# Gathering id blocks one tile a slot instead of four at once, in a graph layer followed by a mixture of experts

## The chip, the cores and the metric

The kernel runs on one core of a Trainium2 chip. The core has five engines, each with an instruction queue of its own that it works off strictly in order: TensorE (PE; its weight loads are listed as PEld), VectorE (DVE), ScalarE (ACT), GpSimd (POOL) and SyncE (SP, which only issues DMAs here). Engines wait for each other, and for DMAs, by semaphores. The metric is the device time in microseconds. The time before is 1313.23 us, the median of three runs (1313.06 to 1322.8).

## The reference

6250 nodes with 256 features, 100000 edges with 96 features. `dst` names the node that each edge belongs to, and it is sorted. What is computed, cut to what matters:

```python
x1 = layernorm(x)
s, c, m = segment_sum(edge, dst), count(dst), segment_max(edge, dst)   # per node, 0 where c is 0
h = concat([x1, s, m, s / max(c, 1), u[0]])
x = x + relu(h @ W1 + b1) @ W2 + b2 + x1                                # 1024 hidden
y = layernorm(x)
top2 of y @ gate_w + gate_b; weights = softmax(top2 values)
moe = sum over the two experts of weight * (relu(y @ w1[e] + b1[e]) @ w2[e] + b2[e])
out = x + layernorm(y + moe) * gamma + beta
```

All of it is float32.

## The kernel before

**Tiles and groups.** The nodes are cut into 50 tiles of 125, and these into 13 groups: group 0 has two tiles, the others four. Groups go from the last nodes to the first. For each group the kernel builds the transposed input `inT` (`turn`), runs the hidden layer (`hidden`, L766 and L771, eight column blocks) and the output layer (`output`, L779), adds the residual, normalizes (`norm_b`, L806, into the tile `xr`), transposes that for the gate (`turn_b`, L818), picks two experts (`choose`, `rank`, `rank_2`, `place`) and sends each row twice to its expert's place in DRAM (`send`, L891, indirect DMAs on GpSimd: eight for a group of four tiles). `xr` has one buffer, so `norm_b` of a group can write only when the sends of the group before have been read out. The experts' blocks come after all groups, from about 815 us on.

**The edge stream.** The sums and maxima per node come from running sums over the sorted edges. VectorE makes them in chunks (L316 to L320, with ScalarE copying the first item of a region, L312 and L313); SyncE loads the edges (`raw`, L176, three buffers) and stores the running sums (`rows_d`, L329). The edges lie in seven regions. The stores of region 0 go to an address that comes from a register. Over the ends of runs a small chain is made (`over_runs`, `over_partitions`, `to_runs`), whose result GpSimd writes to `carry_d` (L440). A group then gathers its nodes' rows of `rows_d` (`take_edges`, L722, tile `at`) and of `carry_d` (`take_carry`, L729, tile `cg`), with indirect DMAs on GpSimd, and VectorE joins the two (L735 and L737). `keep_x` has a part on ScalarE (L714) and then one on GpSimd (L716).

**The node search.** To know which row of `rows_d` a node needs, the kernel finds the first edge of each node in two steps. `find_block(t)` (L486, ScalarE) compares the nodes of a tile with the first ids of 400 blocks of 250 ids and counts. `take_blocks(a, z)` turns the counts of tiles a to z into block numbers (L490 to L492, three VectorE instructions) and gathers, for each of those tiles, one block of 250 ids for each node (L495, one indirect DMA a tile on GpSimd, tile `gb`, six buffers). `find_edge(t)` (L502, ScalarE) counts within the block. `bounds`, `index_nodes` and `counts` then make the indices. Groups are searched in batches: batch 2 is group 2 (4 tiles), batch 3 is group 3 plus one more (8 tiles), batch 4 has 12 tiles, batch 5 has 20. Batches 0 and 1 are done in the prologue.

**The order of the work.** It is written out by hand. Each task is given a slot with `at_slot`; a group has twelve slots (`SLOTS`), and group g begins in slot 12 g. Tasks are emitted by slot, within a slot in the order in which they were added, and each engine runs its instructions in the order in which they were emitted. A slot is not a time: an engine goes on as soon as its semaphores allow. Between slots, as much of the edge stream is emitted as a credit of 4.6 us a slot allows, less the `cost` that tasks name. For a batch with first slot U, the lines around the change are

```python
for i, t in enumerate(reversed(range(a, z))):
    if b > GW:
        at_slot(U + i, find_block, t)
    at_slot(U + i + GS + 3, find_edge, t)
for t0 in range(z - GS, a - GS, -GS):
    t1 = t0 + GS
    at_slot(U + z - t1 + GS, take_blocks, max(t0, a), t1, cost=0.5)
```

with GS = 4, and U = 0, 6, 26 and 54 for batches 2 to 5. So four gathers each are emitted in slot 4 (batch 2), 10 and 14 (batch 3), 30, 34 and 38 (batch 4), 58, 62, 66, 70 and 74 (batch 5). The tasks of the groups are added before those of the search, so they come first within a slot. GpSimd's other tasks are: `fill_rows` (slot 4, added last; two DMAs of 2088 KB that preset the experts' rows), `keep_x` of groups 1 to 7 (slots 5, 20, 29, 41, 53, 65, 77), `take_edges` and `take_carry` of groups 2 to 7 (from slots 17, 26, 38, 50, 62 and 74 on, over three slots each, two tiles a slot), and `send` of groups 0 to 4 (slots 23, then 35 and 36, 47 and 48, 59 and 60, 71 and 72).

Of the kernel before, what the change touches and what calls it, by code (L numbers as in the profile page):

```python
# [11 lines left out]
I32 = mybir.dt.int32  # L12
# [7 lines left out]
P = 125  # L20
# [9 lines left out]
KB = 250  # L30
GS = 4
# [13 lines left out]
def kernel(  # L45
# [18 lines left out]
    nc = tc.nc  # L64
# [114 lines left out]
    ix = edges.enter_context(tc.tile_pool(name="ix", bufs=1, side="right"))  # L179
# [46 lines left out]
    def load_all_ids():  # L226
        L = L100
        nc.vector.memset(ids100[:, L:], N)
        src = bass.AP(tensor=dst.tensor, offset=dst.offset, ap=[[L, 100], [1, L + WE]])
        nc.scalar.dma_start(ids100[0:99], src[0:99])  # L230
        nc.scalar.dma_start(ids100[99:100, 0:L], src[99:100, 0:L])
# [19 lines left out]
    def limits():  # L251

        nc.vector.tensor_scalar(low, part_i[:100], float(ER // L100), float(P * GRP[GW - 1][0]), op0=OP.is_equal, op1=OP.mult)
        nc.vector.memset(limit, 2.0 * N)
        at_p = ix.tile([100, 1], F32, name="at_p")
        for c in range(len(JR) - 1):
            lo, q = P * GRP[GW + sum(GR[:c + 1]) - 1][0], REG[c][0] // L100 - 1
            assert REG[c][0] % L100 == 0
            nc.vector.tensor_scalar(at_p, part_i[:100], float(q), float(lo - 2 * N), op0=OP.is_equal, op1=OP.mult)
            nc.vector.tensor_add(limit, limit, at_p)  # L260

    def check_order():

        L = L100
        nc.vector.tensor_tensor(viol[:, 0, :], ids100[:, 0:L], ids100[:, 1:L + 1], op=OP.is_gt)
        nc.vector.tensor_tensor(viol[:, 1, :], ids100[:, 0:L], ids100[:, WE:L + WE], op=OP.is_equal)
        nc.vector.scalar_tensor_tensor(viol[:, 1, :], ids100[:, 0:L], float(P * GRP[GW - 1][0]), viol[:, 1, :],
                                       op0=OP.is_ge, op1=OP.mult)

    def check_fit():  # L270
        L = L100
        red = ix.tile([100, 3], F32, name="red")
        nc.vector.tensor_reduce(red[:, 0:1], viol.rearrange("p h k -> p (h k)"), AX.X, OP.max)
        nc.vector.tensor_tensor(red[:, 1:2], ids100[:, L - 1:L], limit, op=OP.is_ge)
        nc.vector.tensor_tensor(red[:, 2:3], ids100[:, 0:1], low, op=OP.is_lt)
        ps_v = eps.tile([P, 3], F32, name="ps")
        nc.tensor.matmul(ps_v, ones[:100, :P], red, start=True, stop=True)
        bad = ix.tile([P, 1], F32, name="bad")
        nc.vector.tensor_reduce(bad, ps_v, AX.X, OP.add)
        nc.vector.tensor_scalar(misfit, bad[0:1, :], 1.0, None, op0=OP.min)  # L280
        nc.vector.tensor_scalar(shift, bad[0:1, :], 1.0, float(EP * JR[0]), op0=OP.min, op1=OP.mult)
        nc.vector.tensor_scalar(nf, bad, 0.0, None, op0=OP.is_equal)
# [168 lines left out]
    def block_starts():  # L451
        nc.vector.tensor_copy(dsf, ids100[:, 0:E // 100].rearrange("p (q k) -> p q k", k=KB)[:, :, 0])
        nc.vector.tensor_tensor(dsx, ident[:100, None, :100].to_broadcast([100, QB, 100]),
                                dsf[:, :, None].to_broadcast([100, QB, 100]), op=OP.mult)
        ps_b = eps.tile([P, NBK], F32, name="ps")
        nc.tensor.matmul(ps_b, ones[:100, :P], dsx.rearrange("p q k -> p (q k)"), start=True, stop=True)
        nc.scalar.copy(b1r, ps_b)
# [5 lines left out]
    blk_i = ix.tile([P, NT], I32, name="blk_i")  # L463
# [4 lines left out]
    def more_constants():  # L468
        nc.vector.tensor_scalar(nhalf, node_i, -0.5, None, op0=OP.add)
        nc.vector.memset(rp[:, NT:], float(E))  # L470
        nc.vector.tensor_scalar(sh, row_i[:P, :P], 1.0, part_i[:P], op0=OP.add, op1=OP.is_equal)
        nc.vector.tensor_scalar(wrap, row_i[:P, :P], float(P - 1), None, op0=OP.is_equal)
        nc.vector.tensor_scalar(wrap, wrap, ident[:P, 0:1], None, op0=OP.mult)
        nc.vector.tensor_scalar(before, row_i, part_i, None, op0=OP.is_gt)
        nc.vector.memset(cnt_f, 0.0)
        nc.vector.memset(M[:, 0, :], 0.0)

    dst_b = dst.rearrange("(b k) -> b k", k=KB)

    def node_cols(b):  # L480
        g0 = sum(IB[:b])
        return GRP[g0 + IB[b] - 1][0], GRP[g0][1]

    def find_block(t):
        junk = ix.tile([P, NBK], BF16, name="junk")
        nc.scalar.activation(junk, b1r, AF.Sign, scale=-1.0, bias=nhalf[:, t:t + 1], accum_out=acc1[:, t:t + 1])  # L486

    def take_blocks(a, z):
        cols = slice(a, z)
        nc.vector.tensor_scalar(blk_f[:, cols], acc1[:, cols], float(NBK), 0.5, op0=OP.add, op1=OP.mult)  # L490
        nc.vector.tensor_scalar(blk_f[:, cols], blk_f[:, cols], -1.0, 0.0, op0=OP.add, op1=OP.max)
        nc.vector.tensor_copy(blk_i[:, cols], blk_f[:, cols])  # L492
        for t in reversed(range(a, z)):
            gbs_[t] = ix.tile([P, KB], I32, name="gb", bufs=6)
            nc.gpsimd.indirect_dma_start(out=gbs_[t], out_offset=None, in_=dst_b,  # L495
                                         in_offset=IndirectOffsetOnAxis(ap=blk_i[:, t:t + 1], axis=0))

    gbs_ = {}

# [659 lines left out]
    def at_slot(T, fn, *a, cost=0.0):  # L1159
        tasks.append((T, len(tasks), fn, a, cost))  # L1160
# [85 lines left out]
    for b in range(GW, len(IB)):  # L1246

        a, z = node_cols(b)
        U = max(0, SLOTS * (sum(IB[:b]) - 1) - 10 - (z - a))
# [3 lines that stand above are left out]
            at_slot(U + i + GS + 3, find_edge, t)  # L1253
        for t0 in range(z - GS, a - GS, -GS):
            t1 = t0 + GS
            at_slot(U + z - t1 + GS, take_blocks, max(t0, a), t1, cost=0.5)
        T = max(0, SLOTS * sum(IB[:b]) - (9 if b == GW else 12))
        at_slot(T, bounds, b, cost=0.4)
        at_slot(T + 1, index_nodes, b, cost=4.0)
        at_slot(T + 1, counts, b, cost=1.0)  # L1260
# [13 lines left out]
    def loads_1():  # L1274
        take_x(0)
        nc.sync.dma_start(w1x, w1[0:KC * 128].rearrange("(k p) h -> p k h", p=128))
        for q in range(4):
            nc.sync.dma_start(w1r[q * KR:(q + 1) * KR],
                              w1[KC * 128:KC * 128 + KR].rearrange("k (j m n) -> k m j n", m=4, n=128)[:, q])
        take_x(1)  # L1280
        load_ids(0)

    def loads_2():
        nc.gpsimd.dma_start(w1u, w1[D + 3 * EF:D + 3 * EF + GF])
        nc.gpsimd.dma_start(u0, u[0:1].rearrange("a g -> g a"))
        nc.gpsimd.dma_start(b1c, b1.rearrange("(k p) -> p k", p=128))
# [15 lines left out]
    a, z = GRP[0]  # L1302
    a1, z1 = GRP[1]
# [5 lines left out]
    with tc.manual_schedule():  # L1309
        load_all_ids()  # L1310
        loads_1()
        nc.gpsimd.memset(base[0], 0.0)
        loads_2()
        more_constants()
        limits()
        nc.scalar.copy(gap, eps_t[0:1])
        nc.vector.memset(fill, 0.0)
        block_starts()
        check_order()
        for t in reversed(range(a, z)):  # L1320
            find_block(t)
        take_blocks(a, z)
        for t in reversed(range(a1, z1)):
            find_block(t)
        check_fit()
        take_blocks(a1, z1)
        bad_v = nc.values_load(misfit[0:1, 0:1])
    with tc.If(bad_v != 0):

# [163 lines left out]
```

## Time and profile before

| what | value |
|---|---|
| median of three runs | 1313.23 us |
| the profiled execution | 1304.08 us |
| its span, first to last instruction | 1302.3 us |
| PE busy | 1134.1 us (87%) |
| DVE busy | 929.0 us (71%) |
| ACT busy | 646.4 us (50%) |
| POOL busy | 591.3 us (45%) |
| id gathers, L495 POOL, x50 | 67.9 us, 1359 ns each |
| sends, L891 POOL, x100 | 133.4 us, 1334 ns each |
| searches, L502 ACT, x50 | 500 ns each (median) |
| id gathers, from issue to landing | 3.9 / 6.1 / 9.4 us (least, median, most) |

How to read it: the profile gives one execution. Its slices show the busy share of each engine in 40 equal parts of the span, in tenths. A timeline row has the start in us, the duration in us, the engine, the line of the kernel, the operation, what it writes and reads, how many instructions are merged in the row, and in square brackets how long the engine stood idle before it and what ended that. A row of the waits has who waited, for whom, then the sum in us, how often, and the longest. An indirect DMA's time on POOL is that of making its descriptors; the data lands later. "SPq" is SyncE's queue.

### The profile page before, as it was taken

The numbers are of one execution on the slowest core, as the hardware profiler recorded it, in microseconds if no ns is written. First come the engines' busy times: TensorE is split into PE (matmuls) and PEld (weight loads), VectorE is DVE, ScalarE is ACT, GpSimd is POOL, SyncE is SP. The second block draws the span as 40 slices with busy tenths as digits, with TensorE's granted clock in tenths as the row PEclk, the third lists the DMA queues.
The fourth block names the chain that finished last, engine by engine and source line by source line (L and its number), as shares of the span: only waits on it lengthen the run. The fifth ranks groups of instructions, "written<-read, shape, count | busy, mean of one in ns | idle before, by whom it ended". The sixth has DMA issues, their size and how long they took to land.

```text
span 1302.3 us, 16684 instructions
## 1 busy us (share of the span) xinstructions
PE 1134.1 (87%) x4631; PEld 788.7 (61%) x4631; DVE 929.0 (71%) x2465; ACT 646.4 (50%) x1484; POOL 591.3 (45%) x731
## 2 busy tenths in 40 slices
PE   2494899879888879999999999997999999999992
PEld 1262365536545444646465565886888888888882
DVE  4569888869996989989999441444347767776764
ACT  3394256444637452533435333221266766676663
POOL 4122254563466654383643450303046656555664
PEclk9897799889998989989989999998999999999997
DMA  5948876795888897879988311222366777878771
GB/s 161 217 103 237 212 231 183 202 273 149 237 213 260 230 289 192 245 202 257 262 245 241 105 50 62 65 66 81 120 230 223 257 253 262 278 246 270 268 271 70
DMA packets 179473, 260.99 MB, mean 200 GB/s; under 512 B 35915, under 2 KB 145963, under 8 KB 173729
## 3 DMA queue, kind: packets, MB, share of 16 engines
q1 hardware_dynamic: 140241, 202.11, 52.0%
q0 software_dynamic: 39008, 57.22, 15.5%
q8 instruction: 40, 0.66, 0.2%
q14 instruction: 72, 0.59, 0.1%
q10 hardware_dynamic: 112, 0.41, 0.1%
HBM read 146.59 MB, written 121.88 MB: 206 GB/s over the span
## 4 chain that ended last, share of the span: by engine, by line
PE 30%; DMA 8%; DVE 7%; issue 3%; ACT 3%; SPq 2%; POOL 2%; DVEq 0%; POOLq 0%; ACTq 0%
PE acc L1122 9%; PE acc L1142 9%; PE acc L771 6%; DMA eb<-in_eb_dram 5%; PE acc L779 3%; POOL xg_d L891 1%; DMA xt<-in_x_dram 1%; DVE yb L1053 1%; PE pT L1036 1%; ACT yb L1055 1%; DMA rows_d<-rw 1%; DVE bsc L1079 1%; DMA cg<-carry_d,next_i 1%; DVE z L1089 1%; ACT hb L1128 1%
## 5 line engine op out<-in xcount | busy, mean ns | idle before, releaser
L771 PE MATMUL acc<-inT,w1x 128*128 128x500 f32 (+1 forms) x832 | 374.3, 601 | 0.0
L771 PEld LDWEIGHTS acc<-inT,w1x 128*128 128x128 f32 x832 | 162.7, 203 | 184.1 <-issue 182.2
L891 POOL DMA_INDIRECT xg_d<-xr,pos_i x100 | 133.4, 1334 | 241.1 <-DVE xr L886 177.6
L1122 PE MATMUL acc<-xT,wt 128*128 128x256 f32 x912 | 223.9, 389 | 15.2 <-ACT hb L1128 13.6
L1142 PE MATMUL acc<-wt,hb 128*128 128x256 f32 x912 | 206.8, 380 | 0.0
L1122 PEld LDWEIGHTS acc<-xT,wt 128*128 128x128 f32 x912 | 169.8, 192 | 45.9 <-ACT hb L1128 23.0
L1142 PEld LDWEIGHTS acc<-wt,hb 128*128 128x128 f32 x912 | 173.9, 191 | 23.9
L779 PE MATMUL acc<-w2s,hT 128*125 128x256 f32 x800 | 183.6, 386 | 0.0
L773 ACT ACTIVATE hT<-acc,c 128x500 f32<-128x500 f32 (+1 forms) x104 | 68.5, 658 | 226.2 <-PE acc L771 226.0
L779 PEld LDWEIGHTS acc<-w2s,hT 128*125 128x125 f32 x800 | 150.7, 192 | 22.8 <-issue 0.9
L1096 POOL DMA_INDIRECT out_dram<-g,to_i x86 | 95.7, 1113 | 104.2 <-ACT xT L1039 73.0
L1066 POOL DMA_INDIRECT g<-y_d,from_i x86 | 89.9, 1046 | 88.4 <-DVE to_i L1046 51.8
L495 POOL DMA_INDIRECT gb<-in_dst_dram,blk_i x50 | 67.9, 1359 | 131.1 <-DVE blk_i L492 77.6
L1128 ACT ACTIVATE hb<-acc,wt 128x256 f32<-128x256 f32 x200 | 87.9, 465 | 51.7 <-PE acc L1122 51.7
L1055 ACT ACTIVATE yb<-yb,xb 128x256 f32<-128x256 f32 x114 | 51.7, 501 | 103.1 <-DVE yb L1053 101.7
L316 DVE TENSOR_TENSOR rw<-rw,keep 125x768 f32<-125x768 f32 x81 | 77.2, 953 | 11.3 <-DMA rows_d<-rw 9.8
L319 DVE TENSOR_TENSOR rw<-rw,raw 125x768 f32<-125x768 f32 x88 | 83.4, 948 | 0.3 <-DMA raw<-in_edge_dram 0.3
L320 DVE TENSOR_TENSOR rw<-rw,raw 125x768 f32<-125x768 f32 x88 | 83.6, 950 | 0.0
L317 DVE TENSOR_TENSOR rw<-rw,bar 125x768 f32<-125x768 f32 x81 | 82.1, 1013 | 0.0
L756 ACT COPY inT<-pT 128x500 f32<-128x500 f32 (+1 forms) x65 | 35.9, 553 | 89.6 <-PE pT L755 89.5
L722 POOL DMA_INDIRECT at<-rows_d,first_i x44 | 62.5, 1420 | 37.6 <-issue 19.0
L1041 DVE TENSOR_TENSOR xe<-xb,eb 128x512 f32<-128x512 f32 x57 | 39.4, 691 | 55.7 <-DMA eb<-in_eb_dram 55.7
(301 smaller groups left out, 1633.5 us busy)
## 6 DMA issues: line engine op xcount, KB each, us to landing
wt<-in_wpack_dram SPq DMA_DIRECT2D x44, 1026.0 KB
rows_d<-rw SPq DMA_DIRECT2D x46, 960.0 KB
rows_d<-rw SPq DMA_DIRECT2D x46, 540.0 KB
raw<-in_edge_dram SPq DMA_DIRECT2D x46, 480.0 KB
xb<-xg_d SPq DMA_DIRECT2D x57, 261.0 KB
y_d<-yb SPq DMA_DIRECT2D x57, 256.0 KB
raw<-in_edge_dram SPq DMA_DIRECT2D x46, 270.0 KB
xt<-in_x_dram SPq DMA_DIRECT2D x12, 500.0 KB
```

What stands on the lines that cost most here:

```text
L316: nc.vector.tensor_tensor(su, prev[0], keep[c][:, :, s + j, None].to_broadcast(bcast), op=OP.mult)
L317: nc.vector.tensor_tensor(mx, prev[1], bar[c][:, :, s + j, None].to_broadcast(bcast), op=OP.min)
L319: nc.vector.tensor_tensor(su, su, x_j, op=OP.add)
L320: nc.vector.tensor_tensor(mx, mx, x_j, op=OP.max)
L771: nc.tensor.matmul(pH[:, :n * P], w1x[:, k, ms], inT[:, k, :n * P], start=False, stop=(k == KC - 1))
L779: nc.tensor.matmul(pO, G[g]["hT"][m][:, i * P:(i + 1) * P], w2s[:, m, :], start=(m == 0), stop=(m == HC - 1))
L891: d = nc.gpsimd.indirect_dma_start(out=xg_d[:, :], out_offset=IndirectOffsetOnAxis(ap=G[g]["pos"][:, i, k:k + 1], axis=0), in_=G[g]["xr"][ ...
L1066: d = nc.gpsimd.indirect_dma_start(out=g[:, h, :].bitcast(I32), out_offset=None, in_=y_d[:, :], in_offset=IndirectOffsetOnAxis(ap=BL[b]["f ...
L1096: d = nc.gpsimd.indirect_dma_start(out=out[:, :], out_offset=IndirectOffsetOnAxis(ap=BL[b]["to"][:, h:h + 1], axis=0), in_=g[:, h, :], in_ ...
L1122: nc.tensor.matmul(pB[i][:, half, :], wt[:, k * FF + m * 128:k * FF + (m + 1) * 128], xT[:, k, :], start=(k == 0), stop=(k == DC - 1))
L1128: nc.scalar.activation(hb[:, m, :], pB[i][:, half, :], AF.Relu, bias=bias)
L1142: nc.tensor.matmul(pY[:, h, :], hb[:, m, h * 128:(h + 1) * 128], wt[:, W2O + m * D:W2O + (m + 1) * D], start=(m == order[0]), stop=(m == o ...
```

## The change

The three VectorE instructions stay where they were, as `place_blocks`. The gather becomes a task of its own, `take_block(t)`, one a tile. The tile with place i in its batch is gathered in slot U + i + 4, three slots ahead of its search in U + i + 7. So the gathers of batch 2 are emitted in slots 4 to 7, those of batch 3 in 10 to 17, of batch 4 in 30 to 41, and of batch 5 in 58 to 77, one a slot. `take_block` is added last among the batch's tasks, so in its slot it comes behind the groups' tasks and `place_blocks`, and ahead of `fill_rows`. Where the prologue called `take_blocks` it now calls `place_blocks` and then `take_block` for the same tiles in the same order.

```diff
-    def take_blocks(a, z):
+    def place_blocks(a, z):
         cols = slice(a, z)
...
         nc.vector.tensor_copy(blk_i[:, cols], blk_f[:, cols])
-        for t in reversed(range(a, z)):
-            gbs_[t] = ix.tile([P, KB], I32, name="gb", bufs=6)
-            nc.gpsimd.indirect_dma_start(out=gbs_[t], out_offset=None, in_=dst_b,
-                                         in_offset=IndirectOffsetOnAxis(ap=blk_i[:, t:t + 1], axis=0))
+
+    def take_block(t):
+        gbs_[t] = ix.tile([P, KB], I32, name="gb", bufs=6)
+        nc.gpsimd.indirect_dma_start(out=gbs_[t], out_offset=None, in_=dst_b,
+                                     in_offset=IndirectOffsetOnAxis(ap=blk_i[:, t:t + 1], axis=0))
...
-            at_slot(U + z - t1 + GS, take_blocks, max(t0, a), t1, cost=0.5)
+            at_slot(U + z - t1 + GS, place_blocks, max(t0, a), t1, cost=0.5)
+        for i, t in enumerate(reversed(range(a, z))):
+            at_slot(U + i + GS, take_block, t)
...
-        take_blocks(a, z)
+        place_blocks(a, z)
+        for t in reversed(range(a, z)):
+            take_block(t)
```

The prologue's second call, for batch 1, is changed in the same way.

More of the change, by code (lines that the diff above doesn't have):

```diff
@@ L1325 @@
         check_fit()
-        take_blocks(a1, z1)
+        place_blocks(a1, z1)
+        for t in reversed(range(a1, z1)):
+            take_block(t)
         bad_v = nc.values_load(misfit[0:1, 0:1])
```

## The prediction

> **What bounds the kernel now.** I read the page's slices first, then the waits between 220 and 500 us, then GpSimd's timeline, and for each of its DMAs the landing (the last update of its semaphore).
>
> ```profile
> PE   2494899879888879999999999997999999999992
> DVE  4569888869996989989999441444347767776764
> DMA  5948876795888897879988311222366777878771
> ...
> PE pT L818 <- ACT xr L806: 27.1, 12, 10.3
> ...
> DVE at L735 <- DMA cg<-carry_d,next_i: 22.4, 4, 9.0
> ```
>
> A slice is 32.6 us. All id gathers that move lie before 500 us. There neither TensorE nor VectorE is full: in the windows view both are busy 85% of 220 to 480 us, and they wait for each other; the last two lines are where time is lost. TensorE waits for ScalarE's `norm_b` (L806), nearly all of it in three places (275.45: 6.50 us, 396.00: 8.22, 463.57: 10.27); VectorE waits for the carries of `take_carry` (288.3: 9.04, 405.3 and 407.0: 8.67, 474.6: 4.66). After each such place both engines run with hardly a gap to the next one. So the stage is worth what is taken from both, and of two gains at one place the smaller counts.
>
> `norm_b(g)` writes the single buffer `xr`, so it waits for the eight `send`s of group g-1. What stands around those in GpSimd's queue:
>
> ```profile
> 244.47 1.64 POOL L495 DMA_INDIRECT gb<-in_dst_dram,blk_i  x1 [12.68 <-DVE blk_i L492]
> ...
> 249.43 1.45 POOL L495 DMA_INDIRECT gb<-in_dst_dram,blk_i  x1 [0.30 <-issue]
> 251.19 1.22 POOL L891 DMA_INDIRECT xg_d<-xr,pos_i  x1 [0.30 <-issue]
> ...
> 262.83 1.97 POOL L891 DMA_INDIRECT xg_d<-xr,pos_i  x1 [0.21 <-issue]
> ...
> 269.49 1.42 POOL L495 DMA_INDIRECT gb<-in_dst_dram,blk_i  x1 [0.31 <-issue]
> 274.36 1.21 POOL L495 DMA_INDIRECT gb<-in_dst_dram,blk_i  x1 [3.46 <-DMA xg_d<-xr,pos_i]
> ...
> 278.90 1.22 POOL L729 DMA_INDIRECT cg<-carry_d,next_i  x1 [0.30 <-issue]
> ```
>
> Four gathers (6.7 us) stand ahead of the eight sends, and four more with a wait (9.4 us) between the `at` gathers and the first carry. The other two places look alike (367.31 and 391.21; 431.86 and 459.13). The 3.46 us is a lane: GpSimd's DMAs take eight semaphores in turn, and the one eight places back must have landed.
>
> **The change, part by part.** Nothing is added: 13 times three VectorE instructions and 50 gathers as before, the slot's cost of 0.5 kept, so the edge stream is cut in the same places. In the prologue the order is the same. Moved are the 2nd to 4th gather of each chunk, on GpSimd's queue alone (SyncE issues none of them), at about 1.2 + 0.3 = 1.5 us each, 1.7 where DMA is busy.
>
> *(1) Slots 4 to 7, the block of group 2.* Three gathers go behind `fill_rows` and `keep_x(1)`:
>
> ```profile
> 87.65 1.23 POOL L495 DMA_INDIRECT gb<-in_dst_dram,blk_i  x1 [23.27 <-DVE fill L1265]
> ...
> 94.47 2.45 POOL L1267 DMA_DIRECT2D xg_d<-fill  x2
> ...
> 99.14 0.50 ACT L502 ACTIVATE junk<-gb,nhalf 125x250 bf16<-125x250 int32 x1
> ...
> 110.70 1.54 SPq L176 DMA_DIRECT2D raw<-in_edge_dram  x2
> 113.78 7.76 SPq L329 DMA_DIRECT2D rows_d<-rw  x2
> ```
>
> The fill (2 x 2088 KB) now starts at 89.2. In the trace it lands 19.4 us after its start (94.47 to 113.84), so now at 108.6. The next gather, issued at about 94.3, lands after it if the software queue keeps its order. The trace says it does: each `at` gather issued just behind a carry write lands 1 to 2 us after that write (209.80 then 211.91; 464.71 then 466.18). So the search of 99.14 waits until about 109, and behind it on ScalarE stand a search, a mean, the `inT` copy and the first edge copies (L312, L313). From 99.14 that queue needs 5.1 us of work, so the edge copies end at 114.1 instead of 109.2. TensorE would start group 1 one or two us late, which its next waits for VectorE hide (3.68 us at 126.4, 3.08, 1.73). Not hidden: SyncE's load at 110.70 reuses `raw`, waits for those copies, and moves to 114.1, 3.4 us late. Behind it stand six stores of region 0, whose address comes from a register, each issued when the one before has landed (113.78, 120.56, 127.12, 133.56, 139.72, 147.19, last landing 153.88); VectorE's L316 starts at 153.90, after 3.98 us for it. Then come `index_nodes` and the `at` gathers of 161.80. **Cost +3.4 us**; bounds 0 (the fill drains by 105) and +6.
> Here a rule speaks for a smaller cost. The Trainium skill, "DMA: Bandwidth & Descriptors", "Anatomy of one DMA — SWDGE (gpsimd) path", prices a software DMA at 2 us plus its bytes over 436 GB/s: an estimate of 2 + 2 x 4.8 = 11.6 us for the fill, landing at 101, and ScalarE's copies in time: cost 0. The row gives 19.4 us at a DMA share of 0.90 with hardly another transfer running, so I take the row.
>
> *(2) Slot 17, the last gather of group 3's block.* It goes behind the first two `at` gathers of group 2 (161.80, 163.99) and ahead of its carries. VectorE waits for all four of those today (1.70, 0.20, 1.38, 1.10 us), so they arrive 1.5 us later and VectorE with them: **+1.5 us** (bounds 0, +2). Nothing covers it: TensorE already waits 0.52 us there.
>
> *(3) Slots 34 to 40.* Ahead of the last send two gathers instead of four: issued near 259.5 instead of 262.83. That alone is worth little. SyncE's loads and stores, issued from 256.15 to 259.35, hold the engines: sends issued by 256.62 landed by 264.05, all later ones at 273.5 to 274.3. The last two stay behind it, so TensorE gains 0.7. The carries gain more: ahead of the first stands one gather instead of four, and its lane is free at 273.5, so 273.6 instead of 278.90; landing at 282.5 to 283 instead of 288.30. VectorE then meets TensorE's logits (end 287.4) and the later carries (291): 4.2 us earlier. TensorE takes it at 353.67 to 356.8, where it waits 1.75 + 0.20 + 0.84 + 0.57 for VectorE and for what ScalarE makes of VectorE's joins. **-4.2** (bounds 0 and -7).
>
> *(4) Slots 58 to 64.* Sends start at 368.8 instead of 374.01; four leave before the transfers SyncE issues from 373.54, four stay behind them, but with fewer ahead: last landing near 392.3 instead of 394.79. `norm_b` 2.5 to 3 earlier; the carry (lane free at 390) at 391 instead of 398.32, 5.3 us at landing; VectorE then waits for ScalarE's `find_block` (1.37 us at 408.94), so the smaller counts: **-3.0** (bounds 0, -6).
>
> *(5) Slots 70 to 76.* Last send at about 447 instead of 453.42, landing 2 to 2.5 earlier; carry at 459.5 instead of 466.07, so VectorE's 4.66 us go; TensorE gets 2.5 here and the rest at 500.4, where it waits 1.91 us for VectorE: **-4.5** (bounds 0, -8).
>
> *Free of cost:* the searches three slots after their gathers. A slot is 4.7 us, and these gathers land in 3.9 to 9.4 us. The tightest are those behind `keep_x`: that of slot 41 leaves at 290.3 and lands by 299, its search came at 301.71. The gather of slot 59 may land at 389 for a search of 380.69; ScalarE would then sit in `norm_b`'s wait anyway. If that cover is gone, ScalarE's `hT` copies come late, 2 to 5 us a time.
>
> **Sum.** +3.4 + 1.5 - 4.2 - 3.0 - 4.5 = -6.8 us. Against the profiled execution (1304.08, span 1302.3) that is 1297.3; the runs shown have a median of 1313.23, 9.15 above it, and I carry the difference over: **1306.4**.
>
> **Rivals.**
> *The costs are hidden.* The fill drains faster, or SyncE's late load is made up: (3) to (5) at up to 5 us each, no (1): about -13, 1300. For it: every stretch after a long stall has slow matmuls as well (eight L771 at 398.38 took 6.14 us instead of 3.52), not counted above. Against: the serial stores.
> *The gain stays in the DMA queue, and it is slower.* Place: the carries of 270 to 290, with a DMA share of 1.01. If landings are set by when SyncE's transfers end and not by the place in GpSimd's queue, (3) to (5) give 0 to -2, and (1) and (2) stand: +5, 1318. It decides when the carries land less than about 1.6 us earlier per place. For it: four sends issued over 4.5 us landed within 0.8 us. Against: later carries land one by one, some 1.4 us apart.
> *Nothing happens.* VectorE's edge work sets the pace from 180 to 690 us and every shift is given back: 1312 to 1314. Against: VectorE's 22.4 us of waits for carries.
>
> **How the numbers follow.** Likeliest 0.50 (own range -12 to -1: 1301 to 1312), costs hidden 0.24, slower 0.16, nothing 0.10. The range takes the ends of the second and third: 1297 to 1319. One per cent, about what a measurement of this kernel tells from no change, is 13 us: faster by more, below 1300, half of the second case and a fifth of the first, for the matmuls that a long stall no longer slows, 0.22; slower by more, above 1326, only if (1) goes past its bound and no gain comes, 0.07; within, 0.71.
>
> **What would show it.** (1) right: a ScalarE wait of some 10 us before L502 near 99 us, SyncE's first L176 near 114, L316 near 157. (2): the carries of group 2 later than (1) explains. (3) to (5): fewer microseconds in "DVE at L735 <- DMA cg" and "PE pT L818 <- ACT xr". Wrong: those two unchanged, or L502 waiting for late gathers after 220 us.

## The result, and the profile after

The changed kernel takes 1319.61 us, median of 20 runs (1311.37 to 1328.21), against 1313.1 for the kernel before (20 runs, 1305.5 to 1322.8): a ratio of **1.0052, 95% interval 1.0031 to 1.0073**, so 6.8 us slower (0.0052 x 1313.1). The forecast was 6.8 us faster. The profiled execution has a span of 1320.9 us at a mean granted clock of 0.942 (before: 1302.3, 0.947). Single executions of one kernel differ by 17 us in these runs, and by up to 26 in those further down, so times are compared by ratios, and traces by where groups begin.

The slices of the changed kernel (33.0 us each) look as before:

```profile
PE   2494699889888878989999999997999999999992
DVE  5569689969997968989998441443347666776674
DMA  5956786795889896879998311222366777777871
```

Start of a group's hidden layer on TensorE, in us:

| group | 2 | 3 | 4 | 5 | 6 | 7 | 8 | experts |
|---|---|---|---|---|---|---|---|---|
| before | 188.4 | 242.5 | 310.2 | 368.4 | 430.4 | 497.4 | 556.7 | 822.7 |
| after | 194.5 | 248.6 | 314.5 | 372.7 | 435.0 | 507.3 | 567.6 | 833.9 |
| later by | 6.1 | 6.1 | 4.3 | 4.3 | 4.6 | 9.9 | 10.9 | 11.2 |

So 6 us are lost by group 2, 1.8 come back between groups 3 and 4, nothing between 4 and 6, and 5.3 more are lost between 6 and 7. Step (3) of the forecast lies between groups 3 and 5, step (4) between 5 and 6, step (5) between 6 and 7. One pair of traces is thin ground for such small differences, so here are the same stretches in all traces (us; the runs follow below) whose order from slot 18 on is that of before, and in all six in which batches 4 and 5 are spread as in the change:

| groups | step | forecast | before, batch 2 alone, batch 3 alone | six spread kernels |
|---|---|---|---|---|
| 3 to 5 | (3) | -4.2 | 125.9, 125.2, 125.7 | 123.2 to 124.6 |
| 5 to 6 | (4) | -3.0 | 62.0, 64.0, 68.7 | 59.9 to 62.5 |
| 6 to 7 | (5) | -4.5 | 67.0, 69.5, 64.9 | 72.3 to 74.7 |

A small gain in the first row and a loss in the last stand in all six. In the second row the trace of before is the shortest of its three, so a gain there is not excluded.

The waits of the changed kernel between 220 and 500 us (who waited, for whom: sum, times, longest):

```profile
ACT junk L503 <- DMA gb<-in_dst_dram,blk_i: 28.1, 5, 11.3
DVE at L736 <- DMA cg<-carry_d,next_i: 22.5, 4, 11.8
PE pT L819 <- ACT xr L807: 16.6, 12, 6.9
POOL cg L730 <- DMA carry_d<-ct: 8.2, 2, 4.6
PE acc L780 <- ACT hT L774: 6.9, 2, 6.3
```

(Lines behind 495 have moved by one.) TensorE's wait for `norm_b` did fall, from 27.1 to 16.6 (16.6 to 24.6 in the six spread kernels). VectorE's wait for carries did not: 22.4 and 22.5. The first line is new: ScalarE's searches wait for gathers that land late.

**The first chunk.** GpSimd's timeline, and ScalarE's at the second search:

```profile
88.02 1.23 POOL L496 DMA_INDIRECT gb<-in_dst_dram,blk_i  x1 [23.63 <-DVE fill L1268]
89.25 2.45 POOL L1270 DMA_DIRECT2D xg_d<-fill  x2
...
94.28 1.97 POOL L496 DMA_INDIRECT gb<-in_dst_dram,blk_i  x1 [0.20 <-issue]
```

```profile
109.36 0.50 ACT L503 ACTIVATE junk<-gb,nhalf 125x250 bf16<-125x250 int32 x1 [9.88 <-DMA gb<-in_dst_dram,blk_i]
...
113.57 0.83 ACT L313 COPY rw<-raw 125x768 f32<-125x768 f32 x1
```

The fill was issued at 89.25, and its second half landed at 108.58; the gathers of 94.28 to 98.10 landed at 109.27 to 109.86, and ScalarE stood for 9.88 us. SyncE and VectorE behind it:

```profile
114.43 1.54 SPq L176 DMA_DIRECT2D raw<-in_edge_dram  x2
117.49 8.20 SPq L329 DMA_DIRECT2D rows_d<-rw  x2
```

```profile
159.60 0.96 DVE L316 TENSOR_TENSOR rw<-rw,keep 125x768 f32<-125x768 f32 x1 [4.07 <-DMA rows_d<-rw]
```

The load came at 114.43 instead of 110.70, and the chain of stores then ended with VectorE's L316 at 159.60 instead of 153.90.

**The later chunks: ScalarE.** Two of the searches that wait, with what follows each:

```profile
394.95 0.50 ACT L503 ACTIVATE junk<-gb,nhalf 125x250 bf16<-125x250 int32 x1 [9.94 <-DMA gb<-in_dst_dram,blk_i]
...
398.05 2.93 ACT L807 ACTIVATE xr<-xt,stat 125x512 f32<-125x512 f32 x4 [1.18 <-DMA at<-rows_d,first_i]
...
417.67 0.51 ACT L503 ACTIVATE junk<-gb,nhalf 125x250 bf16<-125x250 int32 x1 [4.79 <-DMA gb<-in_dst_dram,blk_i]
```

```profile
425.25 0.33 PE L756 MATMUL pT<-ident,at 125*128 125x125 f32 x1 [0.86 <-ACT at L743]
```

The first waits for the gather of slot 59, which stands among the sends: issued at 379.87, landed at 394.87. This cost nothing: ScalarE then still stood 1.18 us in front of `norm_b`, whose last send landed at 397.74 (the row names another DMA). Before, it stood 11.24 us in that place:

```profile
395.13 2.93 ACT L806 ACTIVATE xr<-xt,stat 125x512 f32<-125x512 f32 x4 [11.24 <-DMA at<-rows_d,first_i]
```

The second waits for the gather of slot 63 (issued at 405.31), and ScalarE then works without a gap up to the `at` rows that TensorE waits for at 425.25.

**The later chunks: the held carry.** Behind group 6, GpSimd before and after:

```profile
466.07 1.44 POOL L729 DMA_INDIRECT cg<-carry_d,next_i  x1 [0.30 <-issue]
```

```profile
467.26 7.59 POOL L730 DMA_INDIRECT cg<-carry_d,next_i  x1 [4.58 <-DMA carry_d<-ct]
475.15 1.20 POOL L730 DMA_INDIRECT cg<-carry_d,next_i  x1 [0.30 <-issue]
```

A carry's descriptors, 1.44 us before, took 7.59. They ended at 474.85, 1.08 us after VectorE's run of L316 to L320 had ended (473.77); the carry landed at 485.42. VectorE's join waits for it, and so does everything behind:

```profile
472.82 0.95 DVE L320 TENSOR_TENSOR rw<-rw,raw 125x768 f32<-125x768 f32 x1
485.53 2.39 DVE L736 SCALAR_TENSOR_TENSOR at<-cg,cross,at 125x96 f32<-125x96 f32 x1 [11.76 <-DMA cg<-carry_d,next_i]
```

```profile
488.55 0.50 ACT L503 ACTIVATE junk<-gb,nhalf 125x250 bf16<-125x250 int32 x1 [11.29 <-DMA gb<-in_dst_dram,blk_i]
...
489.06 0.66 ACT L774 ACTIVATE hT<-acc,c 128x500 f32<-128x500 f32 x1
...
493.88 0.20 ACT L841 ACTIVATE dv<-dv 125x4 f32<-125x4 f32 x1 [2.86 <-DVE dv L840]
```

```profile
489.76 2.50 PE L780 MATMUL acc<-w2s,hT 128*125 128x256 f32 x5 [6.30 <-ACT hT L774]
```

The gather of slot 75 stands behind the held carry in GpSimd's queue; it was issued at 479.68 and landed at 488.47, and its search made ScalarE wait 11.29 us and TensorE 6.30. But VectorE came later still: at 493.88 ScalarE stood 2.86 us more for it. VectorE left the joins of this carry and the next at 488.61, 5.3 us later than before (478.73) when the 4.6 us are taken off by which group 6 began later. That is the whole 5.3 us of this stretch.

### The profile page after: what moved, and what is told of

Read it like the earlier page. It is cut to its first block, busy times and chain, and to the rows that moved or that the text cites. A ratio compares the mean times of both kernels' runs of the same rounds, so it can differ in the third digit from the quotient of the medians.

```text
span 1320.9 us, 16683 instructions
## 1 busy us (share of the span) xinstructions
PE 1140.6 (86%) x4631; PEld 792.6 (60%) x4631; DVE 931.4 (71%) x2465; ACT 646.5 (49%) x1484; POOL 585.8 (44%) x731
## 5 line engine op out<-in xcount | busy, mean ns | idle before, releaser
L892 POOL DMA_INDIRECT xg_d<-xr,pos_i x100 | 129.0, 1290 | 235.6 <-DVE xr L887 171.8
L496 POOL DMA_INDIRECT gb<-in_dst_dram,blk_i x50 | 71.0, 1420 | 126.7 <-DVE blk_i L492 79.4
L316 DVE TENSOR_TENSOR rw<-rw,keep 125x768 f32<-125x768 f32 x81 | 77.8, 961 | 16.2 <-DMA rows_d<-rw 14.9
L320 DVE TENSOR_TENSOR rw<-rw,raw 125x768 f32<-125x768 f32 x88 | 83.8, 952 | 0.0
L1054 DVE TENSOR_TENSOR yb<-acc,xe 128x512 f32<-128x512 f32 x57 | 39.3, 689 | 58.2 <-PE acc L1143 56.4
```

Of the source, the lines that this page charges most:

```text
L316: nc.vector.tensor_tensor(su, prev[0], keep[c][:, :, s + j, None].to_broadcast(bcast), op=OP.mult)
L320: nc.vector.tensor_tensor(mx, mx, x_j, op=OP.max)
L892: d = nc.gpsimd.indirect_dma_start(out=xg_d[:, :], out_offset=IndirectOffsetOnAxis(ap=G[g]["pos"][:, i, k:k + 1], axis=0), in_=G[g]["xr"][ ...
```

## The experiments

Ratios are to the kernel before, run beside it on the same chip, with 95% intervals; us is (ratio - 1) times its median there (1313.1, 1310.8, 1307.7, 1307.3 or 1309.0). Rows whose intervals overlap are not told apart for certain.

| kernel | ratio | interval | us |
|---|---|---|---|
| the change | 1.0052 | 1.0031 to 1.0073 | +6.8 |
| batch 2 alone | 1.0025 | 1.0004 to 1.0046 | +3.3 |
| batch 3 alone | 1.0014 | 0.9987 to 1.0041 | +1.8 |
| batches 4 and 5 alone | 1.0011 | 0.9984 to 1.0039 | +1.4 |
| change, batch 2 back | 1.0016 | 0.9993 to 1.0038 | +2.1 |
| change, late searches of batch 2 | 1.0017 | 0.9992 to 1.0042 | +2.2 |
| change, fill later | 1.0094 | 1.0065 to 1.0124 | +12.3 |
| 4 and 5 alone, late searches | 0.9988 | 0.9963 to 1.0014 | -1.6 |
| the same, broken runs | 0.9943 | 0.9913 to 0.9973 | -7.5 |
| before, broken runs | 0.9992 | 0.9964 to 1.0020 | -1.0 |
| before, 4 and 5 one slot earlier | 0.9916 | 0.9891 to 0.9941 | -11.0 |
| before, three chunks earlier | 0.9930 | 0.9902 to 0.9959 | -9.2 |
| the same, two chunks spread | 0.9952 | 0.9931 to 0.9973 | -6.3 |

The three parts run alone add up to +6.5 us; the whole is +6.8. With intervals of some 3 us on each side of each part, that they agree so closely is partly luck.

**Batch 2 put back** (in slot 4 again, the rest as changed):

```diff
-            at_slot(U + i + GS, take_block, t)
+            at_slot(U + i // GS * GS + GS if b == 2 else U + i + GS, take_block, t)
```

> The changed kernel, but the four gathers of batch 2 stay together in slot 4, ahead of the fill; batches 3, 4 and 5 are gathered one tile a slot. Theory (the fill in the queue: batch 2's gathers land behind it, ScalarE waits, SyncE's edge load and the serial stores of region 0 follow): L502's wait of 9.9 us near 99 us is gone, SyncE's first edge load is back near 111, and the time is 1.000 to 1.002 of before. Rival (the late searches of batches 4 and 5 on ScalarE make the loss, batch 2's is covered): 1.005 as with the whole change.

Measured 1.0016. ScalarE's wait near 99 is gone and SyncE's load is back at 110.5, as the theory has it; the rival's 1.005 is outside the interval. A large part of the loss is in batch 2. Its one trace does not show the gain: group 2 begins at 195.0 there, against 190.2 with batch 3 alone, where the order up to that place is the same. Single traces differ by that much.

**Batch 2 alone** (the condition is `b > 2`: only batch 2 is spread):

> The kernel before, with batch 2 alone gathered one tile a slot. Theory of the fill: the wait of ScalarE near 99 us and the load at 114 are there, and the time is 1.004 of before (5 to 6 us). Rival of the late searches: 1.000.

Measured 1.0025. ScalarE waits 9.99 us for a gather, until 110.34, and SyncE's load comes at 115.41. The time is a little under the theory's 1.004, and the rival's 1.000 is just outside the interval.

**Batches 4 and 5 alone** (condition `b < 4`):

> The kernel before, with batches 4 and 5 alone gathered one tile a slot. Theory of the fill: what norm_b gains is lost again to ScalarE's searches and to carries that wait for the carry write, so 0.999 to 1.001. Rival of the late searches: 1.004 to 1.006. The forecast's steps (3) to (5): 0.991.

Measured 1.0011: the forecast's 0.991 and the rival's 1.004 to 1.006 are both outside the interval; the first theory's 0.999 to 1.001 fits. ScalarE waits five times for gathers, 24.3 us. The groups run 2.6 us ahead of the kernel before at group 6 (427.8 against 430.4), then lose 5.9 on the way to group 7 (72.9 us against 67.0).

**Batch 3 alone** (condition `b != 3`):

> The kernel before with batch 3 alone spread (slots 10 to 17), the last part of the change not yet run by itself. Account of the parts so far: batch 2 alone 1.0025, batches 4 and 5 alone 1.0011, the whole change 1.0052. If the parts add up, this gives 1.0016 (about +2 us, near the +1.5 of the prediction's second step): 1.000 to 1.003. If it costs 1.004 or more, its gathers among the `at` gathers and carries of group 2 cost more than their own 1.5 us; below 1.000, the remainder lies in how batch 2 and the rest act together.

Measured 1.0014; the interval holds zero. In its trace the gather of slot 17 stands at 165.93 between the second `at` gather and the first carry, which comes at 167.57, 1.6 us later measured from the first `at` gather than before (162.25 to 167.57, against 161.80 to 165.49).

**Late searches of batch 2** (the gathers as changed, but three more slots to the search):

```diff
-            at_slot(U + i + GS + 3, find_edge, t)
+            at_slot(U + i + GS + (6 if b == 2 else 3), find_edge, t)
```

> The changed kernel, with the four searches of batch 2 three slots later (slots 10 to 13). The gathers still land behind the fill near 109 us, but ScalarE reaches their searches only after the edge copies. If the loss goes through ScalarE's order: SyncE's first edge load is back near 111 and the time is 1.000 to 1.002. If it goes another way (the fill's own earlier start, the later landing itself): 1.005.

Measured 1.0017, SyncE's load at 110.73. The gathers stand behind the fill as in the change, but the edge copies no longer stand behind their searches on ScalarE. The other reading's 1.005 is outside the interval: most of batch 2's loss goes through ScalarE's order and not through the gathers' own lateness.

**Fill later** (`at_slot(8, fill_rows)` instead of slot 4):

> The changed kernel with fill_rows in slot 8 instead of slot 4, so that all four gathers of batch 2 stand ahead of the fill in GpSimd's queue although each is still issued in a slot of its own. Theory (the fill in front of the gathers is what costs, through ScalarE's wait for them): no ScalarE wait of 10 us near 99, SyncE's first load of region 0 near 111 again, first `at` near 162, ratio to the kernel before 1.000 to 1.003, like the kernel with late searches for batch 2. Rival (the later issue of the gathers itself, or the later searches of batches 4 and 5, make the loss): about 1.005 as in the changed kernel.

Measured 1.0094, worse than both. ScalarE's wait near 99 is gone and the load is early, as expected, but the fill now runs beside the serial stores. SyncE's queue:

```profile
109.48 2.14 SPq L176 DMA_DIRECT2D raw<-in_edge_dram  x2
113.78 19.63 SPq L329 DMA_DIRECT2D rows_d<-rw  x2
133.51 3.77 SPq L176 DMA_DIRECT2D raw<-in_edge_dram  x2
```

The row of 113.78 runs from the issue of one store to the end of the issue of the next, which waits for the landing of the first: 19.63 us instead of 7.76. The first store landed 18.5 us after its issue (132.27) instead of 6.6 (120.41), and the first `at` gather came at 175.1 (before 161.8). The expectation had left out what the fill would meet in its new place.

**Late searches of batches 4 and 5** (the rest as in the kernel before):

```diff
-            at_slot(U + i + GS + 3, find_edge, t)
+            at_slot(U + i + GS + (5 if b > 3 else 3), find_edge, t)
...
-            at_slot(U + i + GS, take_block, t)
+            at_slot(U + i // GS * GS + GS if b < 4 else U + i + GS, take_block, t)
```

> The kernel before with batches 4 and 5 spread as in the change, and their searches two slots later still, five slots behind their gathers. Without the later searches this gave 1.0011, with ScalarE waiting 9.5 and 9.2 us for late gathers. Theory A (those waits ate the gain that the earlier sends and carries brought): they go, and the ratio falls to 0.996 to 0.999. Theory B (the gain is not there, because the carries wait for the landing of the carry write and not for their place in GpSimd's queue): ScalarE's waits go, VectorE's waits for carries stay near 20 us, and the ratio stays within 0.999 to 1.002.

Measured 0.9988. No search waits any more; the waits between 220 and 500 us that are left:

```profile
PE pT L819 <- ACT xr L807: 22.3, 12, 9.1
DVE at L736 <- DMA cg<-carry_d,next_i: 21.5, 6, 7.3
```

The ratio lies in A's band and a hair outside B's, and the carries' waits stayed near 20 us as B has it; the gain over the kernel with waiting searches is 0.0023, less than the intervals can tell. Groups 6 to 7 still take 74.7 us, so that loss is not the searches'. There GpSimd has:

```profile
462.45 6.69 POOL L730 DMA_INDIRECT cg<-carry_d,next_i  x1 [3.73 <-DMA carry_d<-ct]
```

The six kernels with batch 5 spread as in the change (the whole change, batch 2 back, 4 and 5 alone, late searches of batch 2, fill later, this one) have this first carry at 6.0 to 7.6 us. None of the others has it.

**Broken runs.** To test whether VectorE's run holds it, a memset of one number stands after each max of the edge chunks:

```diff
                     nc.vector.tensor_tensor(mx, mx, x_j, op=OP.max)
+                    nc.vector.memset(gap_v, 0.0)
```

> Batches 4 and 5 spread with searches two slots later (0.9988), and on VectorE a memset of one number after each max of the edge chunks (L320), so that the runs of L316 to L320, whose instructions all read two SBUF tiles, are broken every four instructions. In all six kernels with the change's spread of batch 5, the first carry near 465 us took 6 to 7.6 us on GpSimd and ended 1.08 us after such a run of VectorE; group 6 to group 7 took 72.3 to 74.7 us there, 67.0 in the kernel before. Theory (VectorE's unbroken run holds the descriptors back): no GpSimd gather above 5 us, group 6 to 7 near 69, ratio 0.993 to 0.997, less what 88 memsets of some 0.1 us cost. Rival (the long operation comes from something else, such as outstanding DMAs): it stays above 6 us, ratio 0.998 to 1.002.

> The kernel before with the same memset after each L320, nothing else: what the memsets cost or gain by themselves. Its two long GpSimd operations (4.80 us at 444.47, 8.24 at 577.64) end 1.06 and 1.08 us after a run of L316 to L320. Theory: both shrink to below 5 us; ratio 0.995 to 1.002, some 3 to 5 us gained where sends and carries follow, against up to 8 us of memsets, most of them hidden. Rival: both stay, ratio 1.000 to 1.006.

Measured 0.9943 and 0.9992. In the first (the lines here have moved by three), the carry is not held:

```profile
462.36 1.20 POOL L732 DMA_INDIRECT cg<-carry_d,next_i  x1 [3.18 <-DMA carry_d<-ct]
463.86 1.44 POOL L732 DMA_INDIRECT cg<-carry_d,next_i  x1 [0.30 <-issue]
```

Groups 6 to 7 take 68.5 us there, in the range of the order of before, where the six have 72.3 or more. So without the held carry the loss of this stretch is gone; added were only 88 memsets of 59 ns. What that is worth at the end is less sure. The ratios differ by 0.0045 (5.9 us), but their intervals overlap, and in the two traces the lead is made up again by the experts (they begin at 822.9 with the memsets, at 822.0 without). How the memset helps is not shown: in the same trace a later carry is held past one of them (that of 579.58), and in the kernel before with memsets two long operations stay (4.79 and 7.58 us). The theory's "no gather above 5 us" fell.

```profile
576.61 7.58 POOL L732 DMA_INDIRECT cg<-carry_d,next_i  x1 [0.31 <-issue]
```

**Four at once, one slot earlier.** If the place in the queue is to matter, the whole chunk has to be out of the sends' way:

```diff
-        U = max(0, SLOTS * (sum(IB[:b]) - 1) - 10 - (z - a))
+        U = max(0, SLOTS * (sum(IB[:b]) - 1) - 10 - (z - a) - (b > 3))
```

> The kernel before with four gathers at once as before, but batches 4 and 5 begin one slot earlier (chunks in slots 29, 33, 37 and 57, 61, 65, 69, 73), so that the gathers stand neither ahead of the eight sends nor between the `at` gathers and the carries. Queue theory (the prediction's: the place in GpSimd's queue sets sends and carries): TensorE's waits for norm_b fall from 27 to near 10 us and VectorE's for carries from 22 to near 8, time 8 to 12 us less, ratio 0.991 to 0.994. Landing theory (sends gain, carries wait for the landing of the carry write): norm_b's waits fall, those for carries stay at 18 us or more, ratio 0.996 to 1.000; and where the chunk of slots 37 and 73 comes ahead of the carry write, the carries may come later than before.

Whole batches begin earlier, so `find_block` and `find_edge` move with the gathers. Measured 0.9916, the fastest kernel here. The waits of 220 to 500 us:

```profile
PE pT L818 <- ACT xr L806: 5.6, 4, 4.9
DVE at L735 <- DMA cg<-carry_d,next_i: 3.6, 1, 3.6
```

Both fell, so the landing theory, which had the carries' wait at 18 us or more, fell as put: once the sends are out early, the carry write behind them is early too (landed 271.36 instead of 277.27), and with it the carries.

**Only the three chunks ahead of sends earlier:**

```diff
-            at_slot(U + z - t1 + GS, take_blocks, max(t0, a), t1, cost=0.5)
+            S = U + z - t1 + GS
+            at_slot(S - (S in (34, 58, 70)), take_blocks, max(t0, a), t1, cost=0.5)
```

> The kernel before with only the three chunks that stand ahead of sends (slots 34, 58 and 70) put one slot earlier, each still four gathers at once; the chunks between the `at` gathers and the carries (slots 38, 62, 74) stay. Landing theory: what stands between the `at` gathers and the carries lies in the time in which the carry write lands anyway and costs nothing, so this is as fast as the kernel with all chunks one slot earlier or faster, 0.994 to 0.999, with norm_b's waits down to 10 to 18 us. Queue theory: the carries stay late, half the gain of the other, 0.996 against 0.992.

Measured 0.9930, not to be told from 0.9916, and a little better than either theory's band. TensorE's wait for `norm_b` is 4.9 us, VectorE's for carries 11.3. Moving the four gathers away from the sends is most of the gain. With them the slot's `cost` of 0.5 moves, and so where the edge stream is cut; no run separates the two.

**The same, with chunks 38 and 74 spread:**

```diff
-            at_slot(U + i + GS, take_block, t)
+            S = U + i // GS * GS + GS
+            at_slot(U + i + GS if S in (38, 74) else S - (S in (34, 58, 70)), take_block, t)
```

The searches of those two chunks come two slots later, and `place_blocks` stands where its gathers need it.

> The kernel with the three chunks ahead of sends one slot earlier (0.993), and beside it the chunks of slots 38 and 74 spread one gather a slot, their searches two slots later than in the change. No gather stands among the sends. Theory (what decides is whether the eight sends get out before the transfers that SyncE issues; a gather behind them costs only what is late for its search): 0.990 to 0.996, norm_b's waits below 15 us. Rival (spreading by itself costs, since the gathers stand between the carries and land late in the backlog): 0.997 or more, with VectorE's waits for carries back at 20 us.

Measured 0.9952, inside the theory's band. TensorE's waits for `norm_b` are 5.9 us, VectorE's for carries 10.1, not the rival's 20. Spreading behind the sends does not undo the gain, and does not add to it.

**What the sends depend on.** In the traces of before, of the change and of the two fast kernels, take the last of a group's eight sends, the load that SyncE issues in that stretch (L176), and TensorE's wait for `norm_b` (a dash: none above 1 us):

| place | kernel | last send | load | send behind load | wait |
|---|---|---|---|---|---|
| slots 34 to 40 | before | 262.83 | 256.15 | 6.7 | 6.5 |
| | change | 265.57 | 261.87 | 3.7 | 3.5 |
| | one slot earlier | 261.03 | 262.65 | -1.6 | - |
| | three chunks | 257.96 | 257.49 | 0.5 | - |
| slots 58 to 64 | before | 385.67 | 373.54 | 12.1 | 8.2 |
| | change | 386.37 | 377.67 | 8.7 | 6.9 |
| | one slot earlier | 374.99 | 369.68 | 5.3 | 4.9 |
| | three chunks | 373.65 | 368.83 | 4.8 | 4.1 |
| slots 70 to 76 | before | 453.42 | 444.59 | 8.8 | 10.3 |
| | change | 449.39 | 448.28 | 1.1 | 4.0 |
| | one slot earlier | 434.42 | 437.98 | -3.6 | - |
| | three chunks | 433.89 | 437.87 | -4.0 | - |

Within each place these four rank alike by the last two columns. It is a trend and not a rule: with batches 4 and 5 alone, with and without late searches, the last send of the first place is 3.7 us behind the load, as in the change, and the waits are 6.5 and 4.8 us. A send issued ahead of the load lands in 4 to 9 us (the last one of the first place, one slot earlier: 261.03, landed 266.08); one issued 2 us or more behind it in 9 to 15. Of the four gathers in front of the sends the change leaves one there and one among them, so its last sends still fall behind the load.

## Why the prediction was wrong

**Right: what is late in the first chunk.** Fill landing at 108.6 forecast, 108.58 measured; edge copies ending at 114.1, measured 114.40; SyncE's load at 114.1, measured 114.43; a wait of 10 us, 9.88. The chain from the load to L316 had been taken to shift as it stands (157); it grew as well, to 159.60. By the runs step (1) is +3.3 us (batch 2 alone; 0.5 to 6.0) against +3.4 forecast. The rule of the Trainium skill that was set aside there ("DMA: Bandwidth & Descriptors", "Anatomy of one DMA — SWDGE (gpsimd) path") would have given cost 0; its landing at 101 did not come.

**Right, but small: step (2).** +1.8 us by the runs (-1.7 to 5.4) against +1.5: the size agrees, and zero is not excluded.

**Wrong: steps (3) to (5), step (5) above all.** -11.7 forecast, +1.4 measured (-2.1 to 5.1). Comparisons below take off the 6.1, 4.3 and 4.6 us by which groups 3, 5 and 6 began later; times in brackets are as in the traces. The sends' part came: TensorE got `norm_b` 4.0, 1.4 and 5.3 us earlier in the three places, where 0.7, 2.5 to 3 and 2.5 had been put down. What failed is what follows:

- **Step (5), the carry.** Forecast was a carry issued at 459.5, by its place in the queue and its lane, with descriptors as short as before, so that VectorE's 4.66 us go. Two things came between. The carry also waits for the landing of the carry write, which was on record (464.71); it left at 462.7 (467.26), 3.2 us later than forecast. And its descriptors took 7.59 us instead of 1.44, a term put at nothing. VectorE left the joins 5.3 us later instead of earlier, and -4.5 became +5.3 in this trace; all six spread kernels lose in this stretch. With the carry not held (broken runs) the stretch takes 68.5 us: the loss is gone, but the forecast gain is not there either.
- **Step (3), the joins.** The first carry came as forecast (landing at 282.3, 288.44 in the trace; 282.5 to 283 had been put down), but VectorE left the two joins only 1.8 us earlier, not 4.2. VectorE stood 2.79 us more for the second carry (by the semaphore it waits for; the row names nothing), and the join, 0.3 us by itself, lasted 3.08, until GpSimd's `keep_x` was done (rows in the last section). Before, it had lasted 1.88 for the same reason; the prediction had this hold in no step. It is not all of it: in four other spread kernels these joins ended 4 to 5 us earlier relative to the group, and groups 3 to 5 still took only 1 to 3 us less. What took the rest is open.
- **Step (4), the cover of the searches.** "Free of cost: the searches three slots after their gathers" rests on landings of 3.9 to 9.4 us. The view gives these for 11 of the 50 gathers, those whose records it can match; by the last update of its semaphore the slowest of the kernel before took 12.4 us (391.21, landed 403.65). For slot 59 the cover that was named held. For slot 63 there was none: TensorE reached its output layer 2.5 us earlier (415.89 against 414.06), as forecast, then waited for what stands behind that search on ScalarE (0.56 us for `hT`, 0.86 and 0.69 for `at`), and at 426.43 was 0.3 us late (421.78). With no search waiting the whole time fell by 0.0023, within the intervals, so this loss is small or covered by others.

Of the rivals, the slower one (+5, 1318) came nearest in number, for its (1) and (2) as put; that (3) to (5) came out near its 0 to -2 is partly luck, since the held carry was not in it. Its mechanism, landings set by SyncE's transfers, fits the sends in the table. The carries come earlier as soon as the sends are out earlier, and then the forecast's -11.7 is nearly reached, by another edit (-11.0).

**Open:** what decides whether a gather of GpSimd slips through VectorE's run or is held; how the memset changed it; and what limits the gain of step (3).

## What to carry to other kernels

In these traces a small DMA of GpSimd was as late as the large transfers it was issued behind (a gather behind the fill: 15.0 us to its landing; alone: 4). Before moving one, look up which transfer is ahead of it at its new place, on its own queue and on SyncE's, and move it clear of that as a whole. Half out of the way, it gave nothing here. Then ask for each thing behind it what else that waits for: the carries had the carry write and VectorE's run, the joins had `keep_x`, and the searches had no room in ScalarE's order.

## What the runs showed of the hardware

**Some of GpSimd's indirect DMAs last until VectorE's run is over.** The fourteen traces each hold 225 DMA operations of GpSimd that start between 60 and 800 us, with a median of 1.22 to 1.26 us. Of all these, 31 take more than 3.5 us (3.74 to 8.24), and all 31 end 1.06 to 1.09 us after the end of a run of L316 to L320, whose instructions read two SBUF tiles each. In the kernel before:

```profile
583.85 0.95 DVE L320 TENSOR_TENSOR rw<-rw,raw 125x768 f32<-125x768 f32 x1
584.72 0.95 DVE L436 TENSOR_TENSOR tmp<-ps,kp 125x768 f32<-125x768 f32 x1
```

```profile
577.64 8.24 POOL L729 DMA_INDIRECT cg<-carry_d,next_i  x1 [0.30 <-issue]
```

The carry of 577.64 ends at 585.88, 1.08 us after L320 (584.80), while L436, one of whose inputs is `ps`, the output of a matmul, goes on beside it. That the run holds the descriptors is a reading of this coincidence; the memsets did not settle it. The Trainium skill, "SBUF — State Buffer", "Who interferes with whom", says that a VectorE instruction with two SBUF inputs contends with GpSimd instructions that read SBUF. It also reports that `tensor_tensor` was not seen to stall a DMA, and infers as the reason that making descriptors needs the write interface alone. These traces agree with the first and speak against the second where the DMA takes its row numbers from a tile, as all 31 do. Most such operations under the same instructions take only 1.4 us, so it is not a rule that every one is held.

**GpSimd's `keep_x` holds VectorE's joins.** A first join (L735) takes 0.31 us as a rule. In the fourteen traces 38 of 616 took more than 0.6 us (0.65 to 3.48), and all 38 ended 0.11 to 0.13 us after a `keep_x` of GpSimd had ended. Behind group 3, before and then after the change:

```profile
287.70 2.37 POOL L716 TENSOR_TENSOR xt<-xt,b2b 125x1024 f32<-125x1024 f32 x1
...
288.32 1.88 DVE L735 SCALAR_TENSOR_TENSOR at<-cg,cross,at 125x96 f32<-125x96 f32 x1 [9.04 <-DMA cg<-carry_d,next_i]
```

```profile
291.87 3.08 DVE L736 SCALAR_TENSOR_TENSOR at<-cg,cross,at 125x96 f32<-125x96 f32 x1 [2.79 <-issue]
...
292.47 2.35 POOL L717 TENSOR_TENSOR xt<-xt,b2b 125x1024 f32<-125x1024 f32 x1
```

Both read SBUF tiles. The first join ends at 290.20 and `keep_x` at 290.07; in the second pair it is 294.95 and 294.82.

**The fill delays stores as well.** With 4.2 MB of preset rows on GpSimd's queue beside it, SyncE's first store landed in 18.5 us instead of 6.6, though it is on another queue.
